# Moving attention scores, gate terms and nonzero counts from TensorE to VectorE in a four-layer graph network

## The chip, the cores and the metric

The kernel runs on one core of a Trainium2 chip. The time is device time in microseconds (us) from the first to the last instruction. The engines are named as the profile names them: PE is TensorE, PEld its weight loads, DVE VectorE, ACT ScalarE, POOL GpSimd and SP SyncE, which issues DMA transfers. A program on one core lets a single run's state be judged only against other runs of the same kernel; except for two profiled runs of one kernel (counts alone: one slow, one of unknown state), all runs compared here were in the fast state.

## The reference, cut to what matters

The graph has 2,708 nodes with 512 features; `adj` is a 2,708 x 2,708 matrix with many zeros.

```python
deg = jnp.maximum((adj != 0).astype(jnp.float32).sum(-1), 1.0)
x = _layernorm(x + _L0_gnn_ref(x, adj))          # first sweep over adj
x = _layernorm(x + _L1_gnn_ref(x, adj, adj, ...))  # second sweep
x = _layernorm(x + _L2_gnn_ref(x, adj, weight))    # three sweeps (adj @ p)
x = _layernorm(x + _L3_gnn_ref(x, adj, deg, W, b)) # last sweep

def _L1_gnn_ref(x, adj_a, ...):                  # x is x1, the first layer's result
    attn_a = sigmoid(concat([adj_a @ x, x]) @ Wa.T + ba)   # gate a; gate b likewise
    h = x @ W_sa
    scores = (h @ a_sa[0, :Hd])[:, None] + (h @ a_sa[0, Hd:])[None, :]
    e = where(adj_a != 0, exp(-leaky_relu(scores, 0.01)), 0.0)
    ...
```

Two things of this matter here. Each row of x1 needs four dot products of 512 terms: two scores (with `W_sa` folded into the vectors beforehand) and the x part of two gates. And each row of `adj` needs the number of its nonzero entries, which only the last layer uses.

## The kernel before

The kernel goes through the matrix in six sweeps, one for each product with it. A sweep has four ranges of 384, 384, 256 and 330 output columns for each half of the nodes (the first sweep in another order, with 256 first). A range consists of matmuls whose moving operands are tiles of the matrix and sums of such tiles (`s`, `a`), which VectorE forms in place; the products land in four accumulators, and their sums leave PSUM by evictions called W, C, U and P1c. The tiles live in one ring of buffers. In what follows S0r3 is the first sweep's fourth range and S1r0 the second sweep's first.

Scores in the first sweep: a row tile of x1 is transposed (c) and multiplied with four vectors (d).

```python
def c(w=w, got=got):
    got["xT"] = transposed(got["o"], w)                  # 4 transposes on TensorE, copy on ScalarE

def d(t=t, lo=lo, w=w, got=got):
    ps = bank("pg", [P, 4])
    for c in range(DC):
        nc.tensor.matmul(ps[:w], got["xT"][:, c, :w], vmat[:, c, :], start=c == 0, stop=c == DC - 1)
    ... # 7 small VectorE operations
    for m in range(2):                                   # score rows, 128 single floats each
        nc.gpsimd.dma_start(out=SROW[R0, h][m : m + 1, lo : lo + w].rearrange("a i -> i a"),
                            in_=rcol[:w, t, m : m + 1])
```

Counts in the second sweep: a mask by VectorE, then matmuls with a column of ones.

```python
def go(ij, k):
    m = mask_tile()                                      # one of six bf16 buffers
    nc.vector.tensor_scalar(m[:w, :n], A[r, ij, k][:w, :n], 0.0, None, ALU.not_equal)

def tally(ij, k):
    for i, q in enumerate(ts):
        nc.tensor.matmul(deg[r][...], m[:w, ...], ones_bf[:w, 0:1], start=..., stop=True)
```

An eviction that adds two results, and the in-place sum of two tiles:

```python
nc.vector.tensor_tensor(d[:, :n], T[t, c][:, :n], o[:, :n], ALU.add)                 # W, C, U, P1c
nc.vector.tensor_tensor(A[r, dst, k][:w, :n], A[r, a, k][:w, :n], A[r, b, k][:w, :n], op)
```

Each piece of work is given a planned position; the compiler's scheduler then puts the instructions of each engine in an order from its own estimate of the times. Where the text says that one instruction stands ahead of another, it is the order in which the trace shows them.

Of the kernel before, what the change touches and what calls it, by code (L numbers as in the profile page):

```python
# [24 lines left out]
P = 128  # L25
# [16 lines left out]
def wt(k):  # L42
    return min(P, NH - k * P) if k < KT else P
# [3 lines left out]
def gnn_kernel(ctx: ExitStack, tc: tile.TileContext, x, adjT, w_sa, a_sa, w_gcn, b_gcn, wab, bab, w_hop, w_out,  # L47
# [31 lines left out]
    wab_sb = const.tile([P, 2 * DC, 2], F32, name="wab_sb")  # L79
    bab_sb = const.tile([P, 2], F32, name="bab_sb")  # L80
    vmat = const.tile([P, DC, 4], F32, name="vmat")

    def feature(nm):
        return [dram.tile([wt(t % KT), D], F32, name=f"{nm}{t}", tag=f"{nm}{t}") for t in range(NT)]
# [21 lines left out]
    def nat(nm):  # L106
        return pool.tile([P, D], F32, name=nm, tag="nat", bufs=6)

    def mask_tile():
        return pool.tile([P, 384], BF, name="mask", tag="mask", bufs=6)  # L110

    def bank(nm, shape=None):
        return psum.tile(shape or [P, D], F32, name=nm, tag="x", bufs=8)
# [4 lines left out]
    def at(pos, fn):  # L118
        events.append((pos, len(events), fn))
# [286 lines left out]
    def transposed(dsts, w):  # L406
        ps = bank("ps_t", [P, DC, P])
        for c in range(DC):
            nc.tensor.transpose(ps[:, c, :w], cols(dsts, c)[:w], ident[:w, :w])  # L409
        t = pool.tile([P, DC, P], F32, name="xT", tag="xT", bufs=2)  # L410
        nc.scalar.copy(t[:, :, :w], ps[:, :, :w])
        return t
# [7 lines left out]
    def fetch(src, nm="ld"):  # L420
        t = nat(nm)
        nc.sync.dma_start(out=t[: src.shape[0]], in_=src)
        return t
# [4 lines left out]
    S = [28.0 * s for s in range(8)]  # L428



    row, run, rd = {}, {}, {}
    cnt = {}

    def tiles_of(R0, n):
        return list(range(R0 // P, (R0 + n + P - 1) // P))
# [110 lines left out]
    def done0(p0, dp, last, R0, n, h, C, tiles):  # L547
        for i, (t, lo, w) in enumerate(tiles):
            got = {}

            def a(t=t, got=got):
                got["x"] = fetch(X0[t])

            def b(t=t, lo=lo, w=w, got=got):
                ps = untranspose(C, h, lo, w)
                y = got["x"]
                nc.vector.scalar_tensor_tensor(y[:w], ps[:w], rd[t][:w], y[:w], ALU.mult, ALU.add)
                o = targets(t, last and not h, "o")
                layernorm(o, y, w, not last)
                store(X1[t], o, w)  # L560
                got["o"] = o

            def c(w=w, got=got):
                got["xT"] = transposed(got["o"], w)

            def d(t=t, lo=lo, w=w, got=got):
                ps = bank("pg", [P, 4])
                for c in range(DC):
                    nc.tensor.matmul(ps[:w], got["xT"][:, c, :w], vmat[:, c, :], start=c == 0, stop=c == DC - 1)
                q = slice(t, t + 1)  # L570
                nc.vector.tensor_scalar(neg_s[:w, q], ps[:w, 1:2], -1.0, None, ALU.mult)
                nc.vector.tensor_scalar(neg_s01[:w, q], ps[:w, 1:2], -0.01, None, ALU.mult)
                nc.vector.tensor_tensor(gate_x[:w, t, :], ps[:w, 2:4], bab_sb[:w], ALU.add)

                s = small.tile([P, 2], F32, name="s")
                nc.vector.tensor_copy(s[:w, 0:1], ps[:w, 0:1])
                nc.vector.tensor_scalar(s[:w, 1:2], ps[:w, 0:1], 0.01, None, ALU.mult)
                nc.vector.tensor_tensor(g_col[:w, q], s[:w, 0:1], s[:w, 1:2], ALU.max)
                nc.vector.tensor_tensor(rcol[:w, t, :], g_col[:w, q].to_broadcast([w, 2]), s[:w], ALU.subtract)
                for m in range(2):  # L580
                    nc.gpsimd.dma_start(out=SROW[R0, h][m : m + 1, lo : lo + w].rearrange("a i -> i a"),
                                        in_=rcol[:w, t, m : m + 1])

            p = p0 + dp * i
            at(p - 0.3, a)
            at(p, b)
            at(p + 0.5, c)
            at(p + 0.65, d)

    def start0():  # L590
        ws = load_w(w_sa, KT)
        nc.scalar.dma_start(out=wab_sb, in_=wab)
        nc.scalar.dma_start(out=bab_sb, in_=bcast(bab, 2))
        y = nat("vy")
        for n in range(2):
            v = nat("va")
            nc.scalar.dma_start(out=v, in_=bcast(a_sa[:, n * D : (n + 1) * D], D))
            for c in range(DC):
                nc.vector.scalar_tensor_tensor(y, ws[c], 1.0, v, ALU.mult, ALU.mult,
                                               accum_out=vmat[:, c, n : n + 1])  # L600
        for c in range(DC):
            nc.vector.tensor_copy(vmat[:, c, 2:4], wab_sb[:, DC + c, :])

    def x0_load(k, s):
        if s == "B12":
# [5 lines left out]
    for k in range(KT):  # L611
# [4 lines left out]
        at(-3.0 + 0.3 * f, lambda k=k: x0_load(k, "B22"))  # L616
        at(6.2 + 0.9 * f, lambda k=k: x_sums(k))
        at(7.5 + f, lambda k=k: x_last(k))
    at(2.6, start0)
    sweep(S[0], KT, RANGES0, prep=prep0, extra=extra0, done=done0, first=True, sums=True)  # L620


# [11 lines left out]
    at(S[1] - 1.0, start1)  # L634
    deg = {}

    def extra1(pb, r, R0, n, A):
        ts = list(range(R0 // P, (R0 + n + P - 1) // P))

        masks = {}  # L640

        def go(ij, k):
            h = int(ij[0]) - 1
            w = wt(k)
            m = mask_tile()
            nc.vector.tensor_scalar(m[:w, :n], A[r, ij, k][:w, :n], 0.0, None, ALU.not_equal)
            masks[ij, k] = m

        def tally(ij, k):
            h = int(ij[0]) - 1  # L650
            w = wt(k)
            m = masks.pop((ij, k))
            first = ij == "11" and k == 0
            if first:
                deg[r] = bank("deg", [P, 8])
            for i, q in enumerate(ts):
                wq = wt(q)
                nc.tensor.matmul(deg[r][:wq, 4 * h + i : 4 * h + i + 1], m[:w, q * P - R0 : q * P - R0 + wq],
                                 ones_bf[:w, 0:1], start=first and i == 0, stop=True, skip_group_check=True)

        for ij, p in (("11", -0.6), ("21", 0.05), ("22", 1.05), ("12", 3.6)):
            for k in range(KT):
                at(pb + p + 0.8 * k / KT, lambda ij=ij, k=k: go(ij, k))
                at(pb + p + 0.8 * k / KT + 0.12, lambda ij=ij, k=k: tally(ij, k))

        def end():
            for h in range(2):
                for i, q in enumerate(ts):
                    wq = wt(q)
                    o = rdeg[:wq, h * KT + q : h * KT + q + 1]  # L670
                    nc.vector.tensor_scalar(o, deg[r][:wq, 4 * h + i : 4 * h + i + 1], 1.0, None, ALU.max)
                    nc.vector.reciprocal(o, o)
                    nc.gpsimd.dma_start(out=DROW[R0, h][0:1, q * P - R0 : q * P - R0 + wq].rearrange("a i -> i a"),
                                        in_=o)

        at(pb + 5.0, end)

    def done1(p0, dp, last, R0, n, h, C, tiles):
        for i, (t, lo, w) in enumerate(tiles):
# [255 lines left out]
```

## Time and profile before

| | before |
|---|---|
| time | 3254.28 us, median of 4 runs (3254.24 to 3260.02) |
| TensorE busy | 97% of the span |
| VectorE busy | 49% |
| TensorE's waits up to 560 us, longest single ones | 8.4 us (transpose of x1), 5.6 us (C), 4.5 us (P1c) |
| TensorE's waits from 560 to 936 us (second sweep) | none |

The table is to be read from the busy shares and its last row: TensorE sets the end, VectorE is half idle, and in the second sweep TensorE never waits, so there is slack on VectorE there. The prediction shows the lines. What it only quotes in words is the clock around the waits of the first sweep. These are windows of the kernel before: stretch in us, length, then busy time and number of instructions of TensorE, its loads, VectorE, ScalarE and GpSimd, then the granted clock, the DMA share and GB/s.

```profile
80.00:100.00 20.00, 12.93 (x59) 9.71 (x59) 17.80 (x53) 9.12 (x19) 5.42 (x10) 0.74 0.77 247
100.00:120.00 20.00, 16.86 (x87) 13.49 (x88) 13.36 (x48) 9.02 (x19) 8.43 (x15) 0.79 0.88 106
480.00:500.00 20.00, 10.11 (x37) 6.72 (x36) 9.52 (x39) 0.99 (x2) 6.77 (x13) 0.76 0.68 121
500.00:520.00 20.00, 16.40 (x73) 10.25 (x71) 7.71 (x27) 0.00 (x0) 6.75 (x13) 0.81 0.83 90
```

In each of the four TensorE's busy time falls short of 20 us and the clock of 1.00: the first pair lies at the building of the score vectors, the second at the border of the first two sweeps. In windows of 2 us the clock was 0.50 from 82 to 86, from 102 to 108 and from 494 to 506 us, during or after waits of TensorE of 5.6 us (up to 81.3 us), 3.2 (up to 100.7) and 8.4 (up to 497.9). Half clock in these texts means such stretches.

### The profile page before, as it was taken

The page shows a single profiled execution, that of the slowest core. Times are in us where ns is not written, and L with a number is a line of the kernel's source. Part 1 is how long each engine was busy: PE and PEld are TensorE (multiplying, and loading weights), DVE is VectorE, ACT ScalarE, POOL GpSimd, SP SyncE. Part 2 cuts the span into 40 slices and gives each one's busy share as a digit, 9 for nine tenths or more (in the row PEclk, how much of TensorE's full clock was granted, in tenths as well). Part 3 has the DMA queues.
Part 4 walks back from the last instruction along what each step waited for, and adds up shares of the span by engine and source line. Part 5 has one row for each costly group of instructions (what it writes and reads, how often), then busy time and mean ns, then how long its engine had stood idle before and what let it go on. Part 6 is the DMA issues. An engine that isn't in the chain of part 4 may idle for free. (4 is left out here: it accounts for less than half of the span.)

```text
span 3251.8 us, 35410 instructions
## 1 busy us (share of the span) xinstructions
PE 3161.5 (97%) x12090; PEld 2051.8 (63%) x12090; DVE 1593.5 (49%) x3914; ACT 567.2 (17%) x1096; POOL 399.7 (12%) x703
## 2 busy tenths in 40 slices
PE   6899998999999999999999999999999999999998
PEld 5656665556765556765557765568656587555674
DVE  5877685333456675775232342323344343553544
ACT  3553300000044454531000000000000000000000
POOL 1333222000000101112000020000101011300000
PEclk9899998999999999999999999999999999999999
DMA  6768665322343343444323443324534344543340
GB/s 208 192 151 149 150 147 91 74 63 61 81 95 110 111 121 99 143 147 134 107 83 96 120 149 106 97 68 120 149 103 140 102 141 121 172 118 99 93 134 33
DMA packets 258037, 380.42 MB, mean 117 GB/s; under 512 B 35020, under 2 KB 215020, under 8 KB 257856
## 3 DMA queue, kind: packets, MB, share of 16 engines
q1 hardware_dynamic: 214420, 269.20, 31.9%
q0 software_dynamic: 34720, 98.12, 10.6%
q10 hardware_dynamic: 8716, 10.84, 1.1%
q8 instruction: 95, 1.56, 0.2%
q14 instruction: 86, 0.70, 0.1%
HBM read 322.53 MB, written 55.49 MB: 116 GB/s over the span
## 5 line engine op out<-in xcount | busy, mean ns | idle before, releaser
L259 DVE TENSOR_TENSOR a<-a,a 128x384 f32<-128x384 f32 (+4 forms) x963 | 476.5, 510 | 289.2 <-PE accu L292 151.1
L292 PE MATMUL accu<-a,B 128*128 128x384 f32 (+5 forms) x1188 | 368.9, 456 | 0.0
L292 PE MATMUL accd<-a,B 128*128 128x384 f32 (+5 forms) x1188 | 362.6, 452 | 0.0
L292 PE MATMUL acca<-a,B 128*128 128x384 f32 (+5 forms) x1188 | 361.9, 460 | 0.0
L292 PE MATMUL accc<-s,T 128*128 128x384 f32 (+5 forms) x1188 | 359.3, 455 | 0.0
L292 PE MATMUL accd<-a,T 128*128 128x384 f32 (+5 forms) x1188 | 351.3, 452 | 2.0 <-DVE a L259 2.0
L292 PE MATMUL accc<-a,T 128*128 128x384 f32 (+5 forms) x1188 | 352.5, 453 | 0.0
L292 PE MATMUL accu<-a,T 128*128 128x384 f32 (+5 forms) x1188 | 349.8, 452 | 0.0
L259 DVE TENSOR_TENSOR s<-a,a 128x384 f32<-128x384 f32 (+4 forms) x321 | 161.5, 508 | 278.7 <-PE acca L292 94.1
L292 PEld LDWEIGHTS accd<-a,T 128*128 128x128 f32 (+1 forms) x1188 | 223.6, 190 | 114.4 <-DVE a L259 4.4
L292 PEld LDWEIGHTS acca<-a,B 128*128 128x128 f32 (+1 forms) x1188 | 225.3, 193 | 109.3 <-issue 7.8
L292 PEld LDWEIGHTS accu<-a,T 128*128 128x128 f32 (+1 forms) x1188 | 223.5, 190 | 109.6
L292 PEld LDWEIGHTS accc<-a,T 128*128 128x128 f32 (+1 forms) x1188 | 222.2, 190 | 106.2
L292 PEld LDWEIGHTS accd<-a,B 128*128 128x128 f32 (+1 forms) x1188 | 220.3, 190 | 109.2 <-issue 14.4
L292 PEld LDWEIGHTS accu<-a,B 128*128 128x128 f32 (+1 forms) x1188 | 219.5, 191 | 106.1 <-issue 14.5
L292 PEld LDWEIGHTS accc<-s,T 128*128 128x128 f32 (+1 forms) x1188 | 219.8, 190 | 102.6 <-issue 3.9
L374 POOL TENSOR_TENSOR rstd<-rstd,neg_half 128x1 f32<-128x1 f32 (+1 forms) x88 | 51.6, 586 | 965.2 <-DVE rstd L373 959.4
L333 DVE TENSOR_TENSOR W<-W,accd 128x384 f32<-128x384 f32 (+2 forms) x54 | 27.0, 508 | 259.5 <-PE accd L292 258.2
L333 DVE TENSOR_TENSOR C<-U,accc 128x384 f32<-128x384 f32 (+2 forms) x54 | 27.5, 509 | 209.5 <-PE accc L292 208.1
L326 ACT COPY U<-accu 128x384 f32<-128x384 f32 (+2 forms) x54 | 23.9, 443 | 580.8 <-PE accu L292 579.6
L718 ACT ACTIVATE e<-row,neg_s 128x384 f32<-128x384 f32 (+5 forms) x176 | 100.8, 573 | 78.7 <-DVE e L720 29.3
L720 DVE TENSOR_TENSOR e<-e,f 128x384 f32<-128x384 f32 (+5 forms) x176 | 87.7, 505 | 50.0 <-ACT f L719 49.2
(201 smaller groups left out, 3187.4 us busy)
## 6 DMA issues: line engine op xcount, KB each, us to landing
a<-in_adjT SPq DMA_DIRECT2D x560, 192.0 KB
a<-in_adjT SPq DMA_DIRECT2D x280, 165.0 KB
a<-in_adjT SPq DMA_DIRECT2D x273, 128.0 KB
cl<-in_adjT POOLq DMA_DIRECT2D x80, 192.0 KB, 3.8
ld<-X SPq DMA_DIRECT2D x60, 256.0 KB
Y<-y POOLq DMA_DIRECT2D x54, 256.0 KB, 2.6
B<-Y POOLq DMA_DIRECT2D x84, 128.0 KB, 3.4
X<-o POOLq DMA_DIRECT2D x36, 256.0 KB, 3.5
```

The source lines that it names most:

```text
L259: nc.vector.tensor_tensor(A[r, dst, k][:w, :n], A[r, a, k][:w, :n], A[r, b, k][:w, :n], op)
L292: nc.tensor.matmul(B[home, c][:, :n], X[STAT[p], k][:w, c * P : (c + 1) * P], A[r, MOV[p], k][:w, :n], start=bool(start and k == k0), stop ...
L326: nc.scalar.copy(T[nm, c][:, :n], B[home, c][:, :n])
L333: nc.vector.tensor_tensor(d[:, :n], T[t, c][:, :n], o[:, :n], ALU.add)
L374: nc.gpsimd.tensor_tensor(rstd[:w, 1:2], rstd[:w, 0:1], neg_half[:w], ALU.pow)
L718: nc.scalar.activation(e[:w, :n], row[R0, h][0][:w, :n], AF.Exp, bias=neg_s[:w, t : t + 1])
L720: nc.vector.tensor_tensor(e[:w, :n], e[:w, :n], f[:w, :n], ALU.min)
```

## The change

The intent is to take work off TensorE, which is full, and give it to VectorE, which is half idle, in the second sweep. The scores and gate terms become four dot products of each row tile with vectors that were spread over all partitions; the counts become a running sum of masks, added over the partitions by one small matmul at the end of a half. The building of the vectors and the stores of the score rows move with them. Core of the diff:

```diff
@@ first sweep @@
-            def c(w=w, got=got):
-                got["xT"] = transposed(got["o"], w)
-
-            def d(t=t, lo=lo, w=w, got=got):
-                ps = bank("pg", [P, 4])
-                for c in range(DC):
-                    nc.tensor.matmul(ps[:w], got["xT"][:, c, :w], vmat[:, c, :], start=c == 0, stop=c == DC - 1)
-                ... (small operations and two stores of a score row)
-            at(p + 0.5, c)
-            at(p + 0.65, d)
...
+    def spread_v(j):
+        ps = bank("pv")
+        for c in range(DC):
+            nc.tensor.transpose(ps[:, c * P : (c + 1) * P], vmat[:, c, j : j + 1].to_broadcast([P, P]), ident)
+        V[j] = feat.tile([P, D], F32, name=f"V{j}", tag=f"e{KT + 1}_{j}")
+        nc.scalar.copy(V[j], ps)
...
-    at(2.6, start0)
+    at(9.3, start0)
+    for j in range(4):
+        at(11.2 + 0.4 * j, lambda j=j: spread_v(j))
@@ second sweep @@
+    def score(t, w, got):
+        x1 = got[t]
+        junk = nat("vy")
+        for j in range(4):
+            nc.vector.scalar_tensor_tensor(junk[:w], x1[:w], 1.0, V[j][:w], ALU.mult, ALU.mult,
+                                           accum_out=sc[:w, t, j : j + 1])
...
+                def go(t=h * KT + k):
+                    got1[t] = fetch(X1[t])
...
-            m = mask_tile()
-            nc.vector.tensor_scalar(m[:w, :n], A[r, ij, k][:w, :n], 0.0, None, ALU.not_equal)
...
+            if (R0, h) not in deg:
+                deg[R0, h] = d = ring_tile("deg")
+                nc.vector.tensor_scalar(d[:w, :n], a[:w, :n], 0.0, None, ALU.not_equal)
+            else:
+                d = deg[R0, h]
+                nc.vector.scalar_tensor_tensor(d[:w, :n], a[:w, :n], 0.0, d[:w, :n], ALU.not_equal, ALU.add)
```

More of the change, by code (lines that the diff above doesn't have):

```diff
@@ L81, in gnn_kernel @@
     vmat = const.tile([P, DC, 4], F32, name="vmat")
+    sc = const.tile([P, NT, 4], F32, name="sc")
+    nc.vector.memset(sc, 0.0)
     def feature(nm):
@@ L433, in gnn_kernel @@
     cnt = {}
+    V = {}
     def tiles_of(R0, n):
@@ L560, in b @@
                 store(X1[t], o, w)
-                got["o"] = o
-            def c(w=w, got=got):
-                got["xT"] = transposed(got["o"], w)
-            def d(t=t, lo=lo, w=w, got=got):
-                ps = bank("pg", [P, 4])
-                for c in range(DC):
-                    nc.tensor.matmul(ps[:w], got["xT"][:, c, :w], vmat[:, c, :], start=c == 0, stop=c == DC - 1)
-                q = slice(t, t + 1)
-                nc.vector.tensor_scalar(neg_s[:w, q], ps[:w, 1:2], -1.0, None, ALU.mult)
-                nc.vector.tensor_scalar(neg_s01[:w, q], ps[:w, 1:2], -0.01, None, ALU.mult)
-                nc.vector.tensor_tensor(gate_x[:w, t, :], ps[:w, 2:4], bab_sb[:w], ALU.add)
-                s = small.tile([P, 2], F32, name="s")
-                nc.vector.tensor_copy(s[:w, 0:1], ps[:w, 0:1])
-                nc.vector.tensor_scalar(s[:w, 1:2], ps[:w, 0:1], 0.01, None, ALU.mult)
-                nc.vector.tensor_tensor(g_col[:w, q], s[:w, 0:1], s[:w, 1:2], ALU.max)
-                nc.vector.tensor_tensor(rcol[:w, t, :], g_col[:w, q].to_broadcast([w, 2]), s[:w], ALU.subtract)
-                for m in range(2):
-                    nc.gpsimd.dma_start(out=SROW[R0, h][m : m + 1, lo : lo + w].rearrange("a i -> i a"),
-                                        in_=rcol[:w, t, m : m + 1])
             p = p0 + dp * i
@@ L635, in gnn_kernel, with scores_end @@
     deg = {}
-    def extra1(pb, r, R0, n, A):
-        ts = list(range(R0 // P, (R0 + n + P - 1) // P))
-        masks = {}
-        def go(ij, k):
-            h = int(ij[0]) - 1
-            w = wt(k)
-            m = mask_tile()
-            nc.vector.tensor_scalar(m[:w, :n], A[r, ij, k][:w, :n], 0.0, None, ALU.not_equal)
-            masks[ij, k] = m
+    def score(t, w, got):
[4 more added lines that the diff above has]
+                                           accum_out=sc[:w, t, j : j + 1])
+    def scores_end(R0, h, ts):
+        q = slice(h * KT + ts[0], h * KT + ts[-1] + 1)
+        m = len(ts)
+        nc.vector.tensor_scalar(neg_s[:, q], sc[:, q, 1], -1.0, None, ALU.mult)
+        nc.vector.tensor_scalar(neg_s01[:, q], sc[:, q, 1], -0.01, None, ALU.mult)
+        for j in range(2):
+            nc.vector.tensor_scalar(gate_x[:, q, j], sc[:, q, 2 + j], bab_sb[:, j : j + 1], None, ALU.add)
+        s01 = small.tile([P, 4], F32, name="s01", bufs=2)
+        nc.vector.tensor_scalar(s01[:, :m], sc[:, q, 0], 0.01, None, ALU.mult)
+        nc.vector.tensor_tensor(g_col[:, q], sc[:, q, 0], s01[:, :m], ALU.max)
+        nc.vector.tensor_tensor(rcol[:, q, 0], g_col[:, q], sc[:, q, 0], ALU.subtract)
+        nc.vector.tensor_tensor(rcol[:, q, 1], g_col[:, q], s01[:, :m], ALU.subtract)
+        for k in ts:
+            for j in range(2):
+                nc.gpsimd.dma_start(out=SROW[R0, h][j : j + 1, k * P - R0 : k * P - R0 + wt(k)].rearrange("a i -> i a"),
+                                    in_=rcol[: wt(k), h * KT + k, j : j + 1])
+    got1 = {}
+    i = 0
+    for R0, n in RANGES:
+        for h in (1, 0):
+            for k in tiles_of(R0, n):
+                def go(t=h * KT + k):
+                    got1[t] = fetch(X1[t])
+                at(S[1] + 0.2 + i, go)
+                at(S[1] + 0.6 + i, lambda t=h * KT + k, w=wt(k): score(t, w, got1))
+                i += 1
+            at(S[1] + 0.62 + i - 1, lambda R0=R0, h=h, ts=tiles_of(R0, n): scores_end(R0, h, ts))
+    def extra1(pb, r, R0, n, A):
+        ts = tiles_of(R0, n)
         def tally(ij, k):
@@ L651, in tally @@
             w = wt(k)
-            m = masks.pop((ij, k))
-            first = ij == "11" and k == 0
-            if first:
-                deg[r] = bank("deg", [P, 8])
+            a = A[r, ij, k]
+            if (R0, h) not in deg:
[4 more added lines that the diff above has]
+                nc.vector.scalar_tensor_tensor(d[:w, :n], a[:w, :n], 0.0, d[:w, :n], ALU.not_equal, ALU.add)
@@ L656, in tally, with end @@
+        for ij, p in (("11", -0.6), ("21", 0.05), ("22", 1.05), ("12", 3.6)):
+            for k in range(KT):
+                at(pb + p + 0.8 * k / KT, lambda ij=ij, k=k: tally(ij, k))
+        def end(h):
+            d = deg.pop((R0, h))
+            ps = bank("ds", [P, 4])
             for i, q in enumerate(ts):
                 wq = wt(q)
-                nc.tensor.matmul(deg[r][:wq, 4 * h + i : 4 * h + i + 1], m[:w, q * P - R0 : q * P - R0 + wq],
-                                 ones_bf[:w, 0:1], start=first and i == 0, stop=True, skip_group_check=True)
@@ L661, in extra1 @@
-        for ij, p in (("11", -0.6), ("21", 0.05), ("22", 1.05), ("12", 3.6)):
-            for k in range(KT):
-                at(pb + p + 0.8 * k / KT, lambda ij=ij, k=k: go(ij, k))
-                at(pb + p + 0.8 * k / KT + 0.12, lambda ij=ij, k=k: tally(ij, k))
-        def end():
-            for h in range(2):
-                for i, q in enumerate(ts):
-                    wq = wt(q)
-                    o = rdeg[:wq, h * KT + q : h * KT + q + 1]
-                    nc.vector.tensor_scalar(o, deg[r][:wq, 4 * h + i : 4 * h + i + 1], 1.0, None, ALU.max)
-                    nc.vector.reciprocal(o, o)
-                    nc.gpsimd.dma_start(out=DROW[R0, h][0:1, q * P - R0 : q * P - R0 + wq].rearrange("a i -> i a"),
-                                        in_=o)
@@ L676, in extra1 @@
-        at(pb + 5.0, end)
+                nc.tensor.matmul(ps[:wq, i : i + 1], d[:, q * P - R0 : q * P - R0 + wq], ones_f, start=True, stop=True)
+            for i, q in enumerate(ts):
+                wq = wt(q)
+                o = rdeg[:wq, h * KT + q : h * KT + q + 1]
+                nc.vector.tensor_scalar(o, ps[:wq, i : i + 1], 1.0, None, ALU.max)
+                nc.vector.reciprocal(o, o)
+                nc.gpsimd.dma_start(out=DROW[R0, h][0:1, q * P - R0 : q * P - R0 + wq].rearrange("a i -> i a"), in_=o)
@@ L678, in done1 @@
+        at(pb + 2.6, lambda: end(1))
+        at(pb + 5.2, lambda: end(0))
     def done1(p0, dp, last, R0, n, h, C, tiles):
```

## The prediction

> **What bounds the kernel now.** I read the page's busy shares first, then the chain of work that ended last, then the waits of TensorE, then its timeline in the stages that the change touches, and last the windows.
>
> ```profile
> PE 3161.5 (97%) x12090; PEld 2051.8 (63%) x12090; DVE 1593.5 (49%) x3914; ACT 567.2 (17%) x1096; POOL 399.7 (12%) x703
> PE 36%; issue 2%; DMA 1%; DVE 1%; POOL 0%; POOLq 0%; DVEq 0%
> ```
>
> TensorE is busy 97% of the span, VectorE 49%, and the chain (first line busy shares, second line chain) is nearly all TensorE. So an instruction taken off TensorE's queue is worth what it holds the queue, and work on VectorE is free unless TensorE has to wait for it. The exceptions are in the first 560 us. TensorE's waits from the start to 560 us:
>
> ```profile
> PE cnt L463 <- DVE mask L450: 18.3, 19, 3.9
> PE ps_t L409 <- DVE o L381: 9.9, 2, 8.4
> PE cnt L463 <- ACT mask L453: 7.7, 8, 3.2
> PE pr L485 <- POOL r L477: 7.2, 5, 2.5
> PE ps_n L403 <- ACT C L343: 5.6, 1, 5.6
> PE ps_n L403 <- DVE P1c L333: 4.5, 1, 4.5
> PE pg L569 <- ACT xT L411: 3.2, 1, 3.2
> ```
>
> The columns are total us, times, longest. The 18.3 us lie in the first 26 us, where the data come in, and stay. Of the rest, 13.1 us wait for a transpose of x1 or its copy (ps_t and pg), work that the change deletes.
>
> What do the deleted matmuls cost? Their duration misleads, because they overlap; the start-to-start time counts. TensorE's timeline (start, us) in the second sweep, and one score group in the first:
>
> ```profile
> 583.56 0.22 PE L658 MATMUL deg<-ones_bf,mask 128*128 128x1 bf16 x3
> 583.64 1.54 PE L292 MATMUL accu<-a,T 128*128 128x384 f32 x4
> 585.01 0.22 PE L658 MATMUL deg<-ones_bf,mask 128*128 128x1 bf16 x3
> ...
> 162.18 0.95 PE L569 MATMUL pg<-vmat,xT 128*128 128x4 f32 x8
> 162.99 0.57 PE L292 MATMUL accu<-a,B 128*128 128x384 f32 x1
> ```
>
> Three count matmuls plus four main records repeat every 1.45 us. Undisturbed, 52 such records take 16.77 us, 0.3225 each, so four take 1.29: one count group costs 0.16 us, half in itself (0.08) and half in the slower matmul behind it. A score group holds the queue 0.81 us.
>
> [...] three records of 0.163 us each fit into 0.08 us of queue. [...] after the 5.6 us wait at 75.7 us the mean granted clock of 80 to 100 us was 0.74, and after the 8.4 us wait at 489.5 us that of 500 to 520 us was 0.81. [...] the mask took 334 ns (median), a two-tensor operation on 128x384 some 510 to 550. [...] a score row written as 128 single floats took longer to land than a whole 256 KB tile (3.5 us median). Landing of the score-row stores, and one half of the dot products that VectorE already does:
>
> ```profile
> DMA to landing us min/median/max: 7.7/9.8/16.0
> ...
> L599 DVE SCALAR_TENSOR_TENSOR vy<-w,va x8: 691/691/693, 76.4 to 81.5; 128x512 f32<-128x512 f32 x8
> L599 DVE DVE_READ_ACCUMULATOR vy<-w,va x8: 81/81/84, 77.0 to 82.2; 128x1 f32 x8
> ```
>
> **The change part by part: TensorE.**
> Removed, counts: 484 matmuls in 143 groups of the timeline. The time from a group's start to the next matmul sums to 13.45 us, and the slower matmul behind adds 0.08 each, 11.4: together 24.9 us.
> Removed, transposes of x1 for the scores: 22 tiles. From the first of four to the next other matmul the groups sum to 10.7 us (0.44 each, more at half clock).
> Removed, score matmuls: the same reckoning gives 18.4 us for 22 tiles.
> Added: 16 transposes that spread the four vectors over all partitions, 4 groups x 0.44 = 1.8 us. And 22 small matmuls that sum the running counts over partitions: in the timeline three of the like (rs) hold the queue 0.58 to 0.66 us, so 22 x 0.2 = 4.4 us.
> Net: 24.9 + 10.7 + 18.4 - 1.8 - 4.4 = 47.8 us off the busiest queue, 1.5% of the span.
>
> **VectorE.** Start to start is some 0.08 us under the duration. Removed: 176 masks, at about 0.25 us, 43 us in the second sweep; and 7 operations of 0.07 us spacing and 0.15 us length for each of 22 tiles in the first. Added in the second sweep: 168 running sums of two-tensor form (0.47, 0.41 and 0.335 us apart at 384, 330 and 256 columns: 84 x 0.47 + 42 x 0.41 + 42 x 0.335 = 70.8 us) and 8 first masks; and 22 x 4 dot products of 128x512, 0.735 us apart with their accumulator reads, 64.7 us. With the small ends some 99 us more. Is there room? The windows of the second sweep (span, TensorE, its loads, VectorE, ScalarE, GpSimd, clock, DMA):
>
> ```profile
> 560.00:668.00 108.00, 108.00 (x430) 62.75 (x429) 40.67 (x105) 7.07 (x14) 6.13 (x11) 1.00 0.30 72
> 668.00:782.00 114.00, 114.00 (x445) 66.33 (x444) 34.52 (x97) 6.57 (x14) 5.34 (x10) 1.00 0.29 66
> 782.00:852.00 70.00, 70.00 (x364) 54.64 (x363) 27.30 (x88) 5.94 (x14) 4.28 (x8) 1.00 0.39 87
> 852.00:936.00 84.00, 84.00 (x414) 57.59 (x413) 36.05 (x93) 8.13 (x15) 1.62 (x3) 1.00 0.27 74
> ```
>
> VectorE has 138.5 us busy of 376; with 99 more in some 355 us it comes to 67%. TensorE never waits there now. The tightest place is a step of 14.2 us (44 x 0.3225): 11 combinations and 11 running sums at 0.47, one score tile at 2.9, two evictions: 10.3 + 2.9 + 1.0 = 14.2 us. That is just full, but combinations are planned about three quarters of a step before use, so the next lighter step absorbs it. I allow 3 us of new waits.
>
> **Moved.** Building the vectors leaves the start: there VectorE stood 7.5 us waiting for their load and worked 5.9 us, ScalarE waited 4.1 us behind it, and TensorE then waited 5.6 us (ps_n for C), 3.2 (cnt for the mask) and 3.2 (pg), at half clock for about half of 80 to 108 us. These three waits plus some 8 us of half-clock loss make 20 us; behind them stand the next range's counts and loads (DMA share 0.70 to 0.88 there), so I count 11, less 2 for the same work in its new place. The 44 score-row stores leave the first sweep, whose DMA share is 0.5 to 0.9, for the second with 0.3; of 7.6 us of short waits at 195 to 440 us that I suspect behind them I count 3, and 2 for transposes that no longer wait for ScalarE's normalised rows.
>
> At the border of the sweeps TensorE waited 1.45 and 8.4 us for rows to transpose and lost some 6 us to the half clock: 16 us. But the next sweep needs those rows as operands anyway, after about 12 us of other matmuls, so half comes back as a wait elsewhere: I count 8.
>
> Of the transposes and score matmuls (29.1 us, all in the first sweep) I count 22 realised, since VectorE is near full in stretches there (20.0 of 20 us in 440 to 460). Sum: counts 24.9 - 4.4 = 20.5; first sweep 22 - 1.8 = 20.2; start 9; stores and short waits 5; border 8; new waits -3. That is 59.7 us, and 3254.3 - 59.7 = 3194.6, say 3195 us.
>
> **Rivals.**
> First: the second sweep becomes VectorE's. For it: [...] evictions behind bursts of 2.9 us, a full step. Against it: 67% mean load, and the masks' own waits for TensorE (39.9 us in the sweep) vanish. Each range of four would lose perhaps 5 us: 3215 us.
> Second: the first sweep is held by its loads, and what TensorE saves returns as waits for masks or operands. For it: DMA share up to 0.93 in places, waits for data on ScalarE (23.1 us up to 300 us). Against it: TensorE is fully busy over most of 200 to 480 us. Then only the counts and part of the border are won: some 25 us, 3229 us.
> Third: the stalls at the start and the border vanish whole, with their half clock: 47.8 + 20 + 16 + 5, 89 us, 3165 us.
>
> **Range and chances.** The first two rivals together take away some 35 us, the third adds 30. So 3195 us, with 3166 to 3224 holding it 8 times in 10. Two per cent is 65 us, 3189 us, only 6 us beyond my number with a spread of about 20: faster 0.37, within 2% 0.60, slower 0.03 (only if VectorE's order goes badly wrong).
>
> **What would show it.** Right: no count group in the second sweep's timeline and main matmuls 0.3225 us apart without breaks; the span shorter by about 20 us between 560 and 936 us; VectorE near 65 to 70% there; no 5.6 us wait near 76 us and no 8.4 us wait near 490; the clock near 1.00 from 80 to 120 us; fewer TensorE instructions by about 800 records. Wrong: TensorE waiting for combinations (a or s from the operand sums) or evictions (W, C, U, P1c) in the second sweep by over 10 us in sum; a wait at the border of 8 us or more; score-row stores delaying the second sweep's operand loads; a later sweep changed by more than 3 us, which nothing in my account explains.

## The result, and the profile after

| | before | after |
|---|---|---|
| time, median | 3254.28 us (3254.24 to 3260.02, 4 runs) | 3183.33 us (3178.48 to 3186.40, 4 runs) |
| ratio of the fast runs | | 0.9776, 95% interval 0.9759 to 0.9793 |

A ratio is the mean time of one kernel's fast runs over that of the other kernel's fast runs of the same rounds, so it is not quite the ratio of the medians quoted beside it. The changed kernel is 2.24% faster. The number lies inside the predicted range, 11.7 us below the predicted 3195 us.

The busy shares of the changed kernel:

```profile
PE 3109.3 (98%) x11402; PEld 2014.3 (63%) x11402; DVE 1664.8 (52%) x4001; ACT 559.0 (18%) x1078; POOL 397.8 (12%) x703
```

688 TensorE records are gone (12,090 less 11,402; the prediction said about 800), TensorE's busy time fell by 52 us and VectorE's rose by 71 us; TensorE still sets the end. Its waits in the two first sweeps, from the start to 940 us (total us, times, longest):

```profile
PE cnt L465 <- DVE mask L452: 19.2, 20, 3.9
PE pz L703 <- DVE C L335: 9.5, 2, 9.2
PE ps_n L405 <- DVE P1c L335: 7.7, 2, 7.3
PE pz L703 <- DVE P1c L335: 4.1, 4, 2.3
```

The 18.3 us of the start stayed (19.2). The transposes' waits (ps_t, pg) and the one for ScalarE's copy of C are gone. But two lines are new, pz waiting for the evictions C and P1c: pz is the gate matmul of the second sweep. The same windows as before, and the second sweep's four ranges:

```profile
80.00:100.00 20.00, 15.21 (x99) 11.76 (x99) 17.69 (x49) 14.73 (x30) 10.94 (x19) 1.00 0.69 203
100.00:120.00 20.00, 20.00 (x128) 16.18 (x127) 15.18 (x44) 17.24 (x41) 10.27 (x20) 0.91 0.63 176
...
444.00:570.00 126.00, 117.95 (x381) 69.47 (x380) 93.20 (x251) 6.94 (x13) 20.23 (x37) 0.96 0.47 109
570.00:698.00 128.00, 127.45 (x419) 74.57 (x418) 69.47 (x203) 8.44 (x18) 14.99 (x28) 1.00 0.41 78
698.00:806.00 108.00, 96.28 (x396) 74.61 (x395) 59.74 (x185) 6.87 (x16) 10.19 (x19) 0.91 0.51 90
806.00:917.00 111.00, 109.95 (x402) 71.64 (x401) 66.31 (x160) 42.87 (x69) 9.13 (x17) 0.98 0.46 99
```

The start now runs at a clock of 1.00 and 0.91 instead of 0.74 and 0.79. VectorE is busy 288.7 of 473 us in the second sweep, 61%. Yet in the range from 698 to 806 us TensorE lacks 11.7 us and the clock is 0.91: the second sweep, which had no wait before, has some now.

To see where the time went I counted the main matmuls (the products of the sweeps, 9,340 records in both traces) and took the start of the same matmul in each trace as the start of a stage. The gain of a stage is its length before less its length after:

| stage | length before, us | gain, us | TensorE idle before, us | after, us |
|---|---|---|---|---|
| S0r0 | 122.8 | 22.1 | 18.8 | 6.9 |
| S0r1 | 121.1 | 8.3 | 2.7 | 0.2 |
| S0r2 | 124.9 | 13.1 | 4.4 | 0.0 |
| S0r3 | 118.2 | 26.4 | 12.2 | 1.2 |
| S1r0 | 132.2 | 6.0 | 6.7 | 8.1 |
| S1r1 | 131.5 | 4.0 | 0.0 | 0.6 |
| S1r2 | 93.6 | -14.7 | 0.0 | 11.7 |
| S1r3 | 112.5 | 1.5 | 0.0 | 1.1 |
| all later | 2268.6 | 1.4 | | |

(The first matmul starts 0.9 us later than before.) The first sweep gained 69.9 us. The second one lost 3.3 us, although 484 count matmuls had left it. So two questions are open: why the first sweep gained much more than the 42 us that the prediction gave it (20.2 first sweep, 9 start, 5 stores and short waits, 8 border), and where the 17.5 us of the second sweep (20.5 less 3) went.

VectorE's timeline of the changed kernel around the largest new wait (start, us, instruction, in brackets the idle time before it and what ended it):

```profile
763.58 0.41 DVE L335 TENSOR_TENSOR W<-W,U 128x256 f32<-128x256 f32 x1
765.64 0.50 DVE L676 SCALAR_TENSOR_TENSOR deg<-a,deg 128x330 f32<-128x330 f32 x1 [1.65 <-DMA a<-in_adjT]
772.58 0.50 DVE L676 SCALAR_TENSOR_TENSOR deg<-a,deg 128x330 f32<-128x330 f32 x1 [6.43 <-DMA a<-in_adjT]
774.35 0.50 DVE L676 SCALAR_TENSOR_TENSOR deg<-a,deg 128x330 f32<-128x330 f32 x1 [1.27 <-DMA a<-in_adjT]
774.77 0.33 DVE L673 TENSOR_SCALAR deg<-a 128x330 f32<-128x330 f32 x1
775.13 0.50 DVE L676 SCALAR_TENSOR_TENSOR deg<-a,deg 128x330 f32<-128x330 f32 x1
775.55 0.74 DVE L335 TENSOR_TENSOR C<-U,accc 128x256 f32<-128x256 f32 x2
```

And TensorE's timeline of the same kernel there:

```profile
755.45 9.66 PE L294 MATMUL accc<-a,T 128*128 128x256 f32 x44
764.95 1.89 PE L294 MATMUL accd<-a,B 128*128 128x256 f32 x8
776.02 1.02 PE L703 MATMUL pz<-wab_sb,C 128*128 128x2 f32 x4 [9.18 <-DVE C L335]
```

TensorE finished accumulating accc at 765.1 us. VectorE was idle for most of the next ten us and could have evicted C. It did not, because running sums of the next range (330 columns wide; the current one has 256) stood ahead of C in its order, and three of them waited 1.65, 6.43 and 1.27 us for tiles that were still being loaded. So C began at 775.55 us, 10.4 us after its product was finished, and TensorE waited 9.18 us for it. In the kernel before, C stood behind no more than six masks of the next range, as many as there were mask buffers.

### The profile page after: what moved, and what is told of

Read it like the earlier page. It is cut to its first block, busy times and chain, and to the rows that moved or that the text cites. A ratio compares the mean times of both kernels' runs of the same rounds, so it can differ in the third digit from the quotient of the medians.

```text
span 3184.6 us, 34130 instructions
## 1 busy us (share of the span) xinstructions
PE 3109.3 (98%) x11402; PEld 2014.3 (63%) x11402; DVE 1664.8 (52%) x4001; ACT 559.0 (18%) x1078; POOL 397.8 (12%) x703
## 5 line engine op out<-in xcount | busy, mean ns | idle before, releaser
L294 PE MATMUL accu<-a,B 128*128 128x384 f32 (+5 forms) x1188 | 360.6, 452 | 0.0
L294 PE MATMUL accc<-s,T 128*128 128x384 f32 (+5 forms) x1188 | 351.6, 452 | 0.0
L294 PE MATMUL acca<-a,B 128*128 128x384 f32 (+5 forms) x1188 | 351.6, 453 | 0.0
L294 PEld LDWEIGHTS acca<-a,B 128*128 128x128 f32 (+1 forms) x1188 | 224.4, 191 | 112.5 <-issue 4.8
L294 PEld LDWEIGHTS accd<-a,B 128*128 128x128 f32 (+1 forms) x1188 | 220.2, 190 | 109.4 <-issue 14.7
L676 DVE SCALAR_TENSOR_TENSOR deg<-a,deg 128x384 f32<-128x384 f32 (+5 forms) x168 | 84.9, 506 | 105.3 <-DMA a<-in_adjT 103.9
```

Source lines behind the costliest of these rows:

```text
L294: nc.tensor.matmul(B[home, c][:, :n], X[STAT[p], k][:w, c * P : (c + 1) * P], A[r, MOV[p], k][:w, :n], start=bool(start and k == k0), stop ...
L676: nc.vector.scalar_tensor_tensor(d[:w, :n], a[:w, :n], 0.0, d[:w, :n], ALU.not_equal, ALU.add)
```

## The experiments

Theory A: the running sums ahead of the evictions cost the second sweep its gain, whatever else goes on. Rival B: the fetches of x1 rows, or the bursts of dot products, cost it. Theory A2, formed after the first four runs: it takes both, the order and a VectorE that the dot products have made late. For the first sweep: the start, the stores, or the transposes at the border. The gains by stage of all profiled runs against the profiled run of the kernel before, in us:

| run | S0r0 | S0r1 | S0r2 | S0r3 | S1r0 | S1r1 | S1r2 | S1r3 |
|---|---|---|---|---|---|---|---|---|
| changed kernel | 22.1 | 8.3 | 13.1 | 26.4 | 6.0 | 4.0 | -14.7 | 1.5 |
| scores alone | 25.0 | 8.4 | 13.1 | 19.6 | 7.4 | 0.0 | 0.0 | -2.1 |
| counts alone, second look | -2.0 | -0.6 | -2.6 | 10.4 | 0.4 | 4.8 | 4.6 | 4.6 |
| sums pinned | 22.4 | 8.4 | 13.2 | 26.4 | 4.0 | 4.8 | 4.6 | 4.6 |
| fetch by GpSimd | 24.7 | 8.4 | 13.2 | 26.4 | 5.0 | -4.0 | -10.3 | 1.3 |
| short dot products | 25.1 | 8.3 | 13.1 | 26.4 | 2.9 | 4.8 | -1.9 | 4.6 |
| stores late | -4.0 | -0.4 | 0.1 | 3.9 | -4.1 | 0.0 | 0.0 | 0.0 |
| vectors early | 7.8 | 7.8 | 13.2 | 26.4 | 6.1 | 3.3 | -14.3 | 3.2 |
| border late | -1.2 | 0.7 | -1.5 | 14.9 | -3.4 | 0.0 | 0.0 | 0.0 |
| sums and operand sums pinned | 24.6 | 8.4 | 13.1 | 26.4 | 8.9 | 4.8 | 4.6 | 4.6 |
| sums pinned, fetch by GpSimd | 23.5 | 8.6 | 13.1 | 26.4 | 5.0 | 4.8 | 4.6 | 4.6 |

Single stages of the first sweep are not good to better than some 5 us: rows whose first sweep runs the unchanged code (counts alone, S0r0 to S0r2) still differ from the kernel before by up to 2.6 us, and S0r3 by more. In the second sweep unchanged stages repeat to 0.1 us.

The changed kernel was not run again in the rounds of the experiments; the kernel before was. Where a text below sets a run against the changed kernel's 3183.33 us, the ratios to the kernel before give a somewhat different size: for sums pinned a gain of 15.9 us instead of 18.7, for short dot products 14.6 instead of 16.8, for vectors early a loss of 18.2 instead of 15.2.

### Counts alone

The kernel before with the counting alone changed (the part of the diff from `m = mask_tile()` on); scores as before.

```diff
-            m = mask_tile()
-            nc.vector.tensor_scalar(m[:w, :n], A[r, ij, k][:w, :n], 0.0, None, ALU.not_equal)
+                nc.vector.scalar_tensor_tensor(d[:w, :n], a[:w, :n], 0.0, d[:w, :n], ALU.not_equal, ALU.add)
```

> The kernel before with only the counting of nonzero entries changed to running sums on VectorE in the second sweep; the scores stay as transposes and matmuls in the first sweep. Theory A (the running sums of the next range stand ahead of evictions in VectorE's in-order queue and wait there for adjacency tiles, so TensorE waits for the evictions): the first sweep is as before within 2 us, and the second sweep gains about nothing (-4 to +4 us instead of the 20 that leave TensorE); 3250 to 3258 us. Rival B (the second sweep's loss comes from the fetches of x1 rows for the dot products, or from the bursts of dot products): without them the counts save their 20 us; about 3235 us.

Measured: 3225.91 us against 3253.21 us, ratio 0.9915 (0.9898 to 0.9931), 27 us less. The profiled run took 5551 us at a granted clock of 0.556 and is left out. Theory A as stated fails: it wanted 3250 to 3258 us. The order of VectorE is the same as in the changed kernel (13 of the next range's sums ahead of C, 22 ahead of U, in the first two ranges), so the order alone costs nothing. Rival B wanted 3235 us and is nearer, but 9 us off.

### Scores alone

The kernel before with everything of the change but the counting.

```diff
-            at(p + 0.5, c)
-            at(p + 0.65, d)
+            nc.vector.scalar_tensor_tensor(junk[:w], x1[:w], 1.0, V[j][:w], ALU.mult, ALU.mult,
+                                           accum_out=sc[:w, t, j : j + 1])
```

> The kernel before with only the scores and gate terms changed to dot products in the second sweep (with the vectors built later and the score rows stored there); the counts stay masks and matmuls. Theory A: the first sweep gains about 70 us as in the changed kernel, the second sweep changes by no more than 4 us; about 3184 us. Rival B (fetches of x1 rows and bursts of dot products delay TensorE in the second sweep): the second sweep loses about 20 us; about 3204 us.

Measured: 3183.89 us, ratio 0.9786 (0.9771 to 0.9800), 69.3 us less. This is as theory A wanted, and it refutes rival B: fetches and dot products together, without running sums, cost the ranges S1r1 to S1r3 2.1 us. Separately the two parts gain 69.3 and 27.3 us, together 71: some 26 us get lost only where both are present.

### Running sums pinned behind evictions

```diff
                     nc.vector.tensor_tensor(d[:, :n], T[t, c][:, :n], o[:, :n], ALU.add)
+                    evicted[:] = [nc.cur_bb.bb.instructions[-1]]
...
+            behind.append((nc.cur_bb.bb.instructions[-1], evicted[0]))     # after each running sum
...
+    for i, e in behind:                                                    # order only, no wait
+        tc.add_manual_dep(i, e.name, mybir.DependencyInfo(mybir.DependencyClass.NoSync, ...))
```

> The changed kernel with one more ordering rule for the compiler's scheduler and no new wait: each running sum stands, on VectorE, behind the last eviction that was planned ahead of it. Theory A: TensorE's 9.2 us wait for an eviction near 776 us and its smaller ones go, the second sweep regains 12 to 20 us; about 3165 us. Rival B (fetches): the second sweep stays as in the changed kernel; about 3183 us.

Measured: 3164.59 us, ratio 0.9727 (0.9713 to 0.9742), 18.7 us less than the changed kernel's 3183.33. In the trace no sum of the next range stands ahead of C or U any more, and the ranges S1r1 to S1r3 gain 4.8, 4.6 and 4.6 us. The two largest of TensorE's waits up to 940 us are now:

```profile
PE cnt L468 <- DVE mask L455: 19.9, 20, 3.8
PE ps_n L407 <- DVE P1c L336: 10.1, 1, 10.1
```

The first is that of the start, as ever; the second is the border of the sweeps. No pz line is left in that answer. VectorE's own wait in the second sweep shows the mechanism, 14.4 us for loads where the changed kernel had 103.9 (first fence the changed kernel, second this one):

```profile
DVE deg L676 <- DMA a<-in_adjT: 103.9, 33, 9.6
```

```profile
DVE deg L679 <- DMA a<-in_adjT: 14.4, 6, 6.0
```

### Fetches on GpSimd's queue

```diff
-                    got1[t] = fetch(X1[t])
+                    got1[t] = g = nat("ld")
+                    nc.gpsimd.dma_start(out=g[: X1[t].shape[0]], in_=X1[t])
```

> The changed kernel with the x1 rows for the dot products fetched through GpSimd's queue instead of SyncE's, which also issues the operand and adjacency loads. Rival B (the fetches, held up by their buffers, delay the loads behind them in SyncE's queue): the second sweep regains 12 to 20 us; about 3165 us. Theory A (running sums ahead of evictions, whatever the fetches do): stays within 5 us of 3183 us.

Measured: 3187.60 us, ratio 0.9791 (0.9774 to 0.9807), as the changed kernel within 5 us. That the fetches block the loads behind them in SyncE's queue is not the cause; the sums still wait 94.0 us.

### Counts alone, a second look

The same kernel as in the first run, for a trace in an undisturbed state.

> A second look at the kernel with the counts alone changed, since the profiled run of the first look fell in a slow state (clock 0.556) while the timed ones gained 27 us, not the 0 of theory A nor the 20 of rival B. Theory A2 (the running sums of the next range stand ahead of the evictions here too, but that costs time only when VectorE is behind: the dot products make it late with the current range's sums, these hold the ring buffers, and the next range's tiles are asked for too late): the second sweep shows no TensorE wait for an eviction above 1 us and gains about 20 us, the rest of the gain lies at the border of the sweeps. Rival (something other than the sums' place in the queue): waits for evictions of 5 us or more here too, and the gain lies in the first sweep.

Measured: 3232.17 us in the one run, at a clock of 0.99 (a single run, so its state is formally unknown). In the ranges S1r1 to S1r3 TensorE never waits, and they gain 4.8, 4.6 and 4.6 us: as A2 wanted. Not all of A2 came true: in S1r0, at the border, TensorE waits 9.3 us once for the eviction P1c (4.5 us before), so that the whole sweep gains 14.4 us and not 20. VectorE waits for loads in front of running sums even longer than in the changed kernel, but nothing comes of it:

```profile
DVE deg L650 <- DMA a<-in_adjT: 122.0, 58, 8.2
```

The gain beyond the counts lies in S0r3 (10.4 us), before the sweep; the timed runs and this one differ by 6 us, and what these us are is open.

### Short dot products

```diff
-            nc.vector.scalar_tensor_tensor(junk[:w], x1[:w], 1.0, V[j][:w], ALU.mult, ALU.mult,
+            nc.vector.scalar_tensor_tensor(junk[:w, :16], x1[:w, :16], 1.0, V[j][:w, :16], ALU.mult, ALU.mult,
```

> The changed kernel with each dot product over 16 columns in place of 512, a wrong result on purpose; the fetches of whole x1 rows, the running sums and their rule-free order stay. Theory A2 (the dot products' time on VectorE makes the running sums late): the second sweep regains 15 to 22 us and TensorE's waits for evictions there go; about 3163 us. Rival A1 (order alone, whatever VectorE's load): within 4 us of 3183 us. Rival B (the fetches' traffic): within 4 us of 3183 us.

Measured: 3166.56 us, ratio 0.9731 (0.9711 to 0.9750), with a wrong result as intended (relative error 0.029). So 16.8 us come back if VectorE's time for the dot products is taken away while the fetches and the free order stay (the scheduler moved some neighbouring instructions too); in the profiled runs 13.6 of them lie in the second sweep, a little under the 15 to 22 us that A2 wanted, the rest in S0r0. The order is not what gave them back: as in the changed kernel, 13 of the next range's sums stand ahead of C and 22 ahead of U in the first two ranges. A1 and B fail. A2 holds in the time, but S1r2 still loses 1.9 us, and its reason is not shown: with the dot products the score-row stores that follow them moved too (see the end of "Why the prediction was right or wrong"). TensorE's waits of pz for P1c and C up to 940 us sum to 2.6 and 0.9 us instead of 4.1 and 9.5. VectorE still waits for loads in front of its sums:

```profile
DVE deg L676 <- DMA a<-in_adjT: 124.0, 41, 12.5
```

The three lines with 122.0, 124.0 and 103.9 us say the same thing: the length of VectorE's waits told nothing about the harm here. They did harm only when they went on after TensorE had finished the product that the eviction behind them took out. In S1r2, C began 10.4 us after the last of its matmuls in the changed kernel, 1.8 us after it with short dot products and at once with the counts alone, with 12 of the next range's sums found ahead of it in each of the three traces.

### Score-row stores late

```diff
-                for m in range(2):
-                    nc.gpsimd.dma_start(out=SROW[R0, h][m : m + 1, lo : lo + w].rearrange("a i -> i a"), ...)
+                late.setdefault((R0, h), []).append(stores)   # issued where the changed kernel issues them
```

> The kernel before with only the score-row stores moved out of the first sweep, to where the changed kernel issues them; transposes, score matmuls and the early building of the vectors stay. If the stores' traffic was what made operands and x1 rows late in the first sweep: 12 to 18 us less, about 3239 us, and the 8.4 us wait at the border shrinks. If the waits came from the transposes and score matmuls themselves: within 4 us of 3254 us.

Measured: 3255.28 us against 3252.87, ratio 1.0007 (0.9989 to 1.0025). The stores cost the first sweep nothing, although the DMA share was 0.5 to 0.9 there and each of them took some 10 us to land (9.8 us median in the kernel before). Nor did they harm the second sweep of this kernel (0.0 us in S1r1 to S1r3), where masks and not running sums stand ahead of the evictions.

### Vectors built early

```diff
-    at(9.3, start0)
+    at(2.6, start0)
```

> The changed kernel with the four vectors built at the start again, where the kernel before built them. If that building cost the stalls and the half clock of the first 130 us: 11 to 20 us slower, 3195 to 3204 us, and TensorE waits near 76 us return. If those stalls came from the first score transposes: within 4 us of 3183 us.

Measured: 3198.56 us, ratio 0.9832 (0.9812 to 0.9852), 15.2 us slower than the changed kernel. S0r0 gains only 7.8 us instead of 22.1, and the clock from 80 to 120 us falls back to where it was:

```profile
80.00:100.00 20.00, 12.54 (x59) 9.40 (x59) 17.80 (x52) 7.79 (x16) 4.06 (x8) 0.74 0.83 262
100.00:120.00 20.00, 15.15 (x79) 11.31 (x79) 14.19 (x39) 14.75 (x31) 10.74 (x19) 0.83 0.68 190
```

### The border's score work later

The kernel before with the transposes and score matmuls of the last range's six row tiles moved some us into the second sweep.

```diff
             at(p, b)
+            if last:
+                def again(t=t, got=got):
+                    got["o"] = [(fetch(X1[t]), 0, D)]
+
+                p = S[1] + 1.0 + i + (0 if h else 3)
+                at(p, again)
             at(p + 0.5, c)
```

> The kernel before with the transposes and score matmuls of the last range's six row tiles done a little later, inside the second sweep, from fetched x1 rows; nothing is removed from TensorE and the masks stay. Theory D (the transposes at the border held TensorE up waiting for normalised rows, idle and at half clock, and nothing waits in their place): 12 to 22 us less, 3232 to 3242 us. The prediction's own reckoning (half of 16 us comes back as a wait for the next sweep's operands): about 8 us less, 3245 us. Rival (all comes back): within 3 us of 3253 us.

Measured: 3240.94 us against 3251.82, ratio 0.9966 (0.9949 to 0.9983), 10.9 us less. As a time this is just inside theory D's band, as a gain just short of its 12 us, and above the prediction's 8. The 8.4 us wait for a transpose is gone and the one for P1c, 4.5 us before, is 3.2 us; but one of 5.6 us for a count mask, 1.5 us at most before, is new, so a part does come back. What is left, about 11 us, is due to the place of this score work alone, no work having been removed.

### Both pins of the second sweep, and the border's

First the ordering rule together with the fetches by GpSimd:

> The changed kernel with the ordering rule of the running sums and also the x1 fetches on GpSimd's queue. Theory A2: the second sweep is already free of waits with the ordering rule alone (3164.6 us), so the fetches' queue adds nothing: 3162 to 3168 us. Rival (the fetches' hold on SyncE's queue costs something once the order is right): 3155 to 3161 us.

Measured: 3162.78 us, ratio 0.9725 (0.9711 to 0.9740), within 2 us of the rule alone: once the order is right the fetches' queue does not matter.

Then the ordering rule also for the sums of x1 operands:

```diff
         nc.vector.tensor_tensor(new_x("T4", k)[:w], X["B21", k][:w], X["T2", k][:w], ALU.subtract)
+        if evicted:
+            behind.append((nc.cur_bb.bb.instructions[-1], evicted[0]))
```

> The changed kernel with the ordering rule for the running sums and for the operand sums of the x1 rows too, so that the eviction of P1c at the border of the sweeps does not stand behind operand sums that wait for loads. If TensorE's 10.1 us wait for P1c there comes from that order: 6 to 12 us less than the 3164.6 us of the rule for running sums alone, about 3156 us. If the loads of the x1 rows themselves hold TensorE at the border: the wait moves to an operand and the time stays within 3 us of 3165 us.

Measured: 3152.29 us, ratio 0.9693 (0.9679 to 0.9707), 12.3 us below the rule for the running sums alone, and the fastest kernel here; its result is correct. TensorE's wait for P1c at the border fell from 10.1 to 4.5 us. Of the difference the stage S1r0 with the border accounts for 5 us in the profiled runs (8.9 less 4.0) and the first sweep for 2; everything after the second sweep shows another 5. The rule binds the operand sums of the later sweeps too, and TensorE's waits for P1c there fell from 2.5 to 0.6 us; the rest of these 5 us is not explained.

## Why the prediction was right or wrong

Right inside its range, 11.7 us above the measured time, but by two errors that nearly cancel: the first sweep was underrated by 28 us, the second overrated by 21. That the sum fits so well is luck. The class that the prediction held likeliest, within 2%, was missed by 6 us (2% of 3254.3 is 65.1 us, the medians differ by 71.0).

**Counts, 20.5 us.** Right in size. Where nothing else interferes, a range gains 4.8, 4.6 and 4.6 us (sums pinned), so about 19 us over four ranges. The reading of start-to-start times instead of durations (0.16 us for a group of three whose records last 0.22) holds.

**Transposes and score matmuls, 22 of 29.1 us realised, less 1.8.** The discount was wrong. In the middle ranges S0r1 and S0r2 the removed groups held TensorE 14.1 us in the trace before (11 tiles: 9.1 us of matmuls, 5.0 of transposes), and these stages gained 21.4. Nothing was given back; on top of it 7.1 us of idle time fell to 0.2. The second rival (the first sweep held by its loads) is refuted by that.

**Start, 9 us.** Mis-sized: building the vectors early costs 15.2 us. That lies about midway between the 20 us of its three waits and half clock and the "I count 11" that followed, so what was feared behind them, the next range's counts and loads, took back less than was allowed for. (The experiment moves the loads and dot products of `start0` alone; the transposes that spread the vectors stay late.)

**Stores and short waits, 5 us.** The stores, three of these, were worth nothing (ratio 1.0007). The short waits went all the same, 7 us in two stages, so with the transposes and their copies and not with the stores; which of those was not taken apart.

**Border, 8 of 16 us.** Mis-sized: "half comes back as a wait elsewhere" was too much. Moving the score work alone gives 10.9 us, with one new wait of 5.6 us. In the trace of the changed kernel S0r3 and S1r0 gained 32.4 us, of which 11.3 were removed score work (nine groups at their measured lengths) and about 4.8 counts, so 16 are left. A wait of 7.3 us for P1c stands there in place of the former 4.5, so little came back. The third rival, that start and border vanish whole, was nearly true of the first sweep.

**New waits, -3 us.** This is the step that failed in earnest. In S1r1 to S1r3 the sums pinned gain 14.0 us and the changed kernel loses 9.2, so new waits with their half clock (0.50 from 772 to 782 us, around the end of the 9.18 us wait) cost 23.2 us there. The first rival had named it, "evictions behind bursts of 2.9 us", and would have charged 5 us for each range, 20 us; it was set aside, chiefly because VectorE would be busy only 67% of the time. It was busy 61%, less than that, and the waits came all the same. The mean load was the wrong thing to look at. The point is what stands in the queue ahead of an eviction: sums whose tiles land late, in a window of 12 us, with VectorE idle. One of the prediction's own signs of being wrong came true: TensorE's waits for evictions in the second sweep were to stay within 10 us, and pz waited 13.6 us (9.5 and 4.1). One 9.18 us wait stood in a stage that lost 19.3 us against the pinned kernel (4.6 to -14.7), since the clock fell as well (0.91 in that range).

That the loss needs both parts of the change is shown from both sides (dot products shortened: most of the gain back; order fixed: gain back; one of the two parts alone: at most 2.1 us lost in S1r1 to S1r3). What in the score part does the harm is not shown. A2 had it that late sums hold ring buffers and so delay the requests for the next range's tiles. SyncE's waits list a running sum with 0.2 us at most, and the traces speak against it for the three tiles of the 9.18 us wait. SyncE asked for them from 757.4 to 760.8 us, as accc's matmuls freed buffers, the first 7.7 us before the last of these matmuls ended. With short dot products the loads at the same place began just as early, 7.7 us before. But in the changed kernel they took 8.2 to 13.4 us to land, with short dot products 7.3 us at most.

This points to a rival that no run tests: the small stores. In the changed kernel six score-row stores were issued from 757.7 to 760.3 us and landed from 770.9 to 774.1; with short dot products, which end sooner, all of that group had landed by 759.1. Over the second sweep of the changed kernel 75 of the 103.9 us that running sums waited for loads fall into times in which a score-row or count-row store was under way, and such times are 34% of the stage. So the dot products may do their harm through the stores that follow them and not through VectorE's load; the prediction had named "score-row stores delaying the second sweep's operand loads" as a sign of being wrong. This is coincidence in the traces and no proof. The changed kernel with these stores taken out of the second sweep would decide it.

Later sweeps changed by 1.4 us, as the prediction wanted.

## What to carry to other kernels

When work is moved to a half idle engine, look not at its mean load but at what will stand ahead of its urgent instructions, here evictions that TensorE needs soon; an instruction that only gathers statistics and waits for a load must stand behind them, and an ordering rule without a wait was worth 16 to 19 us here, about a quarter of the whole gain. A small buffer that throttles a stream (six masks) may be what kept that order before, though no run changed the number of masks by itself. And work that was taken away from the full engine next to a stall was worth more than its own time here, since idle time and half clock (0.50 from 82 to 86 us at the start and from 494 to 506 us at the border) went with it: the first sweep gained 70 us, where the score work removed from TensorE was 29 and the move of the vectors' building some 15.

The running sum, a comparison and an addition in one instruction, took as long here as a plain sum of two fp32 tiles. In the second sweep of the changed kernel (busy us, mean ns) the two took 500 and 499 ns at 330 columns, 422 and 419 ns at 256:

```profile
L676 DVE SCALAR_TENSOR_TENSOR deg<-a,deg 128x330 f32<-128x330 f32 x38 | 19.0, 500 | 26.9 <-DMA a<-in_adjT 26.4
L676 DVE SCALAR_TENSOR_TENSOR deg<-a,deg 128x256 f32<-128x256 f32 x38 | 16.0, 422 | 29.6 <-DMA a<-in_adjT 29.4
L261 DVE TENSOR_TENSOR a<-a,a 128x330 f32<-128x330 f32 x30 | 14.8, 499 | 7.8 <-PE accu L294 7.6
...
L261 DVE TENSOR_TENSOR a<-a,a 128x256 f32<-128x256 f32 x30 | 11.9, 419 | 1.0 <-PE accu L294 1.0
```
